# First half of the last head pair by way of DRAM, six taps on VectorE instead of TensorE, and a tile normalised and stored in two parts

## Chip, cores and metric

The kernel runs on one core of a Trainium2 chip. The metric is the device time of one execution in microseconds; the median of three runs is compared. All numbers are float32.

## What is computed

The input x is 16 images of 384 channels, 32 by 32 pixels. Two residual layers follow each other:

```
x = x + attention(gn(x))       # 8 heads of 48 channels over the 1024 pixels, softmax, projection, bias
x = x + depthwise_conv(gn(x))  # 7 x 7, padding 3, weights averaged over the four rotations
```

gn normalises groups of 12 channels over all pixels of an image. The convolution has one 7 x 7 filter for each channel: an output pixel is a sum of 49 products, and one of these 49 shifts (dy, dx) is called a tap.

## The kernel before

An image is three tiles of 128 channels by 1024 pixels. The work goes image by image; the convolution of an image runs beside the attention of the next one, on other engines.

Attention: the 8 heads are 4 pairs, so that there are 64 pairs in all (u = 0 to 63; pair 63 is the last of image 15). For each pair and each half of 512 query pixels, eight steps compute scores on TensorE (s_step, L493), ScalarE takes the exponential (L501), and eight steps multiply with v (av_step, L509). v has a column of ones, so that row 48 of each head's 64 rows of the result holds the softmax sum. ScalarE copies the result to the tile o (take, L520). Then o has to be divided by its sums. For the usual pair this goes by way of DRAM, in three steps that lie some microseconds apart: sums_out (L523) has SP write the two sum rows to DRAM and read them back spread over 128 partitions; invert (L532) takes the reciprocal of 16 columns on VectorE, and SP writes it to DRAM and reads it back, each head's row repeated over 64 partitions; divide (L543) multiplies on VectorE. For the last pair divide_at_once (L585) does it for a half in one go: a matmul with a matrix of ones copies the sums over the partitions (L588), VectorE takes the reciprocal of 512 columns (L590) and multiplies (L591). The first half is divided while TensorE projects the pairs 0 and 1 of the last image, the second half in fast_finish (L1274) between the projections of pair 2 and pair 3. After the projection come the residual (L608), the group statistics (groups_on_pe, L318: small matmuls with masks), and the convolution of the last image.

Convolution: a tap is one instruction on VectorE, x1 = x1 + w * shifted xn1 (conv_tap, L640; x1 is the accumulator, which begins as the layer's input, xn1 its normalised copy). Taps of different tiles take turns. Four helpers take work off VectorE. For the tiles in ROWS_ONLY some taps with dx = 0 are products on ScalarE (L621), which POOL adds in by an accumulating DMA (L945). Three tiles are convolved on TensorE, in PE_TILES: (14, 2), (15, 2) and (15, 1), written (image, tile). For these the normalised tile is stored to DRAM (conv_store, L714), read back four times shifted by a row (conv_load, L722), so that 32 channels by 4 rows lie on the 128 partitions, and multiplied with block matrices: one matmul step covers four values of dy for one dx (conv_on_pe, L756). PE_TAPS holds pairs (d0, dx) with d0 = 0 for dy from -3 to 0 and d0 = 1 for dy from 1 to 3. Each such pair is 4 matmuls for each half of 16 rows, and each matmul is two records in the profile. pe_taps leaves out (1, 0) for tile (14, 2), whose taps (1, 0), (2, 0) and (3, 0) are products on ScalarE. In the last image tile 0 has two accumulators (tap_of_two, L908), and sum3 collects its products.

Order: the schedule is manual. Two counters, clock for TensorE and vclock for VectorE, are advanced by written costs; catch_up (L967) fills VectorE with taps until vclock reaches clock, and runs what after(wait, cost, f) has put down once it is due. act_slot (L1078) does the same for what stands in applies on ScalarE. Each engine's queue, SP's and POOL's DMA starts among them, runs in the order in which the program issues it. SP carries sums, inverses and loads of shifted rows; POOL carries the accumulating DMAs and most stores of results; in the last image ScalarE starts half of the loads of shifted rows.

The turn to the last image's convolution is x1_chains (L1085). For image 15 VectorE normalises tile 2 (L360, conv_begin L632), SP stores it, ScalarE normalises tiles 1 and 0 (L364), and then products and taps of tile 0 begin. For image 14 the same function also queues the early products, each with its time. The tile pools hand out a fixed number of buffers in turn: six for x1, six for xn1, five for qk and the shifted rows, two for the inverses (tag "t"), three double banks and two single banks of PSUM.

Of the kernel before, what the change touches and what calls it, by code (L numbers as in the profile page):

```python
# [10 lines left out]
F32 = mybir.dt.float32  # L11
# [5 lines left out]
P = 128  # L17
# [27 lines left out]
def kernel(  # L45
# [64 lines left out]
    def run(general):  # L110
        tag = "g" if general else "f"
        with ExitStack() as stack:
# [33 lines left out]
            ROWS_ONLY[BESIDE] = range(-PAD, PAD + 1)  # L146

# [444 lines left out]

            def proj_part(b, o, ts):
                if o not in pps:
                    pps[o] = psum(f"ps_proj_{b}_{o}")
                for t in ts:
                    lhsT = wp[:, t, o * P : (o + 1) * P] if t < NK else late["w3"][:, o * P : (o + 1) * P]
                    for h in range(2):
                        nc.tensor.matmul(  # L599
                            pps[o][:, h, :],  # L600
                            lhsT=lhsT,
                            rhs=os_[NP * b + t][:, h * HALF : (h + 1) * HALF],
                            start=(t == 0),
                            stop=(t == NP - 1),
                        )
# [26 lines left out]
            def conv_begin(st, b, k, engine):  # L632
                xn1s[b, k] = spare.pop((b, k), None) or new_xn1(b, k)
                st.apply(xn1s[b, k], x1s[b, k], k, engine)
# [79 lines left out]
            def conv_store(b, k):  # L714
                nc.sync.dma_start(xds[b, k][:, PAD * W : (PAD + H) * W], xn1s[b, k])
# [20 lines left out]
            def pe_taps(b, k):  # L736
                return [t for t in PE_TAPS if t != (1, 0) or (b, k) not in ROWS_ONLY]
# [347 lines left out]
            def x1_chains(b, st):  # L1085
# [14 lines left out]
                if b == B - 2:  # L1100

                    vclock -= 5.0
# [3 lines left out]
                    early = [(beside, 0), (beside, -1), (beside, 1), (first, 1), (beside, -2)]  # L1106
# [46 lines left out]
            def finish(u):  # L1153
                sums_out(u)
                if u < U - 1:
                    waiting.add(u)
                    after(6.0 if u % NP == NP - 1 else 9.0, 0.3, lambda: finish2(u))
# [137 lines left out]
            def fast_end(b):  # L1295
                assert not applies
                for key in ("sum2", "sum3"):
# [13 lines left out]
            for b, n0, size in [  # L1311
# [15 lines left out]
                if ending:  # L1327
                    catch_up(clock)
                    divide_at_once(NP * b + NP - 1, 0)
                    vclock += 4.2  # L1330
# [13 lines left out]
                clock += (size * US_STEP + US_TURN) / 2  # L1344
                if n0 // (2 * NT) < (n0 + size) // (2 * NT):
                    finish((n0 + size) // (2 * NT) - 1)
                if ending:
                    catch_up(clock)
                    assert not invs and not waiting
# [94 lines left out]
```

## Time and profile before

| what | us |
|---|---|
| runs | 2911.31, 2907.84, 2912.79 |
| median | 2911.31 |
| profiled execution | 2906.68 |
| its span, first to last instruction | 2904.5 |

The busy time over the whole span, by engine (busy us, share, instructions):

```profile
PE 2894.4 (100%) x11446; PEld 1169.7 (40%) x11446; DVE 2565.6 (88%) x2559; ACT 1461.4 (50%) x1745; POOL 262.0 (9%) x411
```

PE is TensorE's matmuls, PEld its weight loads, DVE is VectorE, ACT is ScalarE, POOL is GpSimd. "DVE L640" is an instruction of line 640 on VectorE; SPq and ACTq are DMA starts in the queues of SP and ScalarE. The granted clock of TensorE was 1.0 of full speed. A few lines of the groups of instructions, with count, busy us and mean ns of one, then the idle time ahead and what ended most of it:

```profile
L640 DVE SCALAR_TENSOR_TENSOR x<-xn,wsym,x 128x930 f32<-128x930 f32 (+9 forms) x2170 | 2363.9, 1172 | 138.8 <-ACT xn L364 138.7
L756 PE MATMUL ps_conv<-sh,mat 128*32 128x480 f32 (+3 forms) x656 | 67.8, 569 | 0.0
L545 DVE TENSOR_TENSOR o<-o,inv 128x1024 f32<-128x1024 f32 x63 | 77.4, 1228 | 69.7 <-DMA inv<-inv 52.9
```

### The profile page before, as it was taken

To read this page: it belongs to the slowest core of one execution; us is meant where nothing else is said; L and a number is where in the kernel's file an instruction comes from. 1 tells how busy PE (TensorE), PEld (TensorE's weight loads), DVE (VectorE), ACT (ScalarE), POOL (GpSimd) and SP (SyncE) were. 2 spreads that over 40 slices of the span, in tenths; PEclk is the share of its full clock that TensorE was granted. 3 is DMA by queue.
4 is the path that set the end of the run, shared out by engine and by line. 5 is a ranking of instruction groups with operands and counts; after the bars stand their busy time and mean duration, and the time that the engine had idled before them with its cause. 6 is when DMAs were issued, how large, how long until landed. Compare 5 with 4: busy or idle time off the path is not lost.

```text
span 2904.5 us, 30161 instructions
## 1 busy us (share of the span) xinstructions
PE 2894.4 (100%) x11446; PEld 1169.7 (40%) x11446; DVE 2565.6 (88%) x2559; ACT 1461.4 (50%) x1745; POOL 262.0 (9%) x411
## 2 busy tenths in 40 slices
PE   9999999999999999999999999999999999999999
PEld 4343343433434343343433434343343433434333
DVE  5313999989899898998989899898998989899997
ACT  2546445464453645545465454645545455454641
POOL 3111004010100101000010100101001010100101
PEclk9999999999999999999999999999999999999999
DMA  7422022220312203012120212213022130212346
GB/s 287 131 26 63 16 36 77 38 67 23 65 33 43 70 21 84 16 35 70 35 71 16 65 41 43 67 24 84 16 36 70 28 77 16 55 50 43 83 125 174
DMA packets 74284, 175.80 MB, mean 61 GB/s; under 512 B 30528, under 2 KB 32464, under 8 KB 72592
## 3 DMA queue, kind: packets, MB, share of 16 engines
q0 software_dynamic: 34336, 114.90, 15.9%
q1 hardware_dynamic: 38080, 55.20, 7.6%
q10 hardware_dynamic: 1712, 3.67, 0.4%
q8 instruction: 92, 1.51, 0.2%
q14 instruction: 64, 0.52, 0.1%
HBM read 118.61 MB, written 28.72 MB: 51 GB/s over the span
## 4 chain that ended last, share of the span: by engine, by line
PE 100%; DVE 0%; ACT 0%; POOL 0%; issue 0%; POOLq 0%
PE ps_s L493 31%; PE acc L509 31%; PE ps_qk L442 17%; PE ps_v L468 9%; PE ps_proj L562 8%; PE ps_conv L756 2%; PE ps_proj L599 1%; PE warm L1182 0%; PE ps_st_x L332 0%; PE ps_sum L588 0%; ACT qk L449 0%; POOL sc_x L353 0%; DVE x L360 0%; DVE x L777 0%; DVE ones_warm L1176 0%
## 5 line engine op out<-in xcount | busy, mean ns | idle before, releaser
L640 DVE SCALAR_TENSOR_TENSOR x<-xn,wsym,x 128x930 f32<-128x930 f32 (+9 forms) x2170 | 2363.9, 1172 | 138.8 <-ACT xn L364 138.7
L501 ACT ACTIVATE e<-ps_s 128x1024 f32<-128x1024 f32 x1024 | 952.5, 1051 | 54.5 <-PE ps_s L493 51.6
L493 PE MATMUL ps_s<-qk 48*128 48x512 f32 x4096 | 914.2, 596 | 1.1 <-ACT qk L449 1.1
L509 PE MATMUL acc<-e,v 128*64 128x512 f32 x4096 | 907.2, 595 | 0.0
L493 PEld LDWEIGHTS ps_s<-qk 48*128 48x128 f32 x4096 | 376.5, 185 | 535.0 <-ACT e L501 257.2
L509 PEld LDWEIGHTS acc<-e,v 128*64 128x64 f32 x4096 | 283.0, 137 | 608.2 <-issue 599.7
L442 PE MATMUL ps_qk<-x,wqk 128*128 128x512 f32 x1152 | 505.7, 595 | 1.0 <-DVE x L360 1.0
L520 ACT COPY o<-acc 128x512 f32<-128x512 f32 x128 | 75.2, 587 | 602.5 <-PE acc L509 602.3
L442 PEld LDWEIGHTS ps_qk<-x,wqk 128*128 128x128 f32 x1152 | 216.1, 190 | 287.1 <-issue 285.7
L468 PE MATMUL ps_v<-wv,x 128*128 128x384 f32 x768 | 252.0, 488 | 0.0
L562 PE MATMUL ps_proj<-o,wp 128*128 128x512 f32 x540 | 234.2, 592 | 0.0
L449 ACT COPY qk<-ps_qk 128x1024 f32<-128x1024 f32 x96 | 96.8, 1009 | 254.1 <-PE ps_qk L442 254.1
L577 POOL DMA_DIRECT2D x<-in_x x45 | 39.3, 872 | 1796.7 <-ACT x L570 1423.1
L468 PEld LDWEIGHTS ps_v<-wv,x 128*128 128x128 f32 x768 | 144.6, 190 | 109.7 <-ACT e L501 12.1
L562 PEld LDWEIGHTS ps_proj<-o,wp 128*128 128x128 f32 x540 | 102.6, 190 | 126.0 <-issue 120.3
L477 ACT COPY v<-ps_v 128x384 f32<-128x384 f32 x128 | 55.1, 483 | 185.6 <-PE ps_v L468 185.6
L570 ACT ACTIVATE x<-ps_proj,bp 128x1024 f32<-128x1024 f32 x45 | 50.2, 1115 | 182.7 <-PE ps_proj L562 182.7
L545 DVE TENSOR_TENSOR o<-o,inv 128x1024 f32<-128x1024 f32 x63 | 77.4, 1228 | 69.7 <-DMA inv<-inv 52.9
L364 ACT ACTIVATE xn<-x,sc_x 128x1024 f32<-128x1024 f32 x47 | 54.9, 1231 | 71.6 <-DMA sc_x<-gr_x 62.4
L756 PE MATMUL ps_conv<-sh,mat 128*32 128x480 f32 (+3 forms) x656 | 67.8, 569 | 0.0
L387 DVE BATCH_NORM_STATS2 bs_all<-xs 128x6 f32<-128x512 f32 x84 | 52.1, 682 | 17.3 <-DMA xs<-in_x 17.1
L458 POOL DMA_DIRECT2D qk<-qk x96 | 47.3, 526 | 116.4 <-ACT qk L449 115.4
(143 smaller groups left out, 565.4 us busy)
## 6 DMA issues: line engine op xcount, KB each, us to landing
x<-in_x POOLq DMA_DIRECT2D x90, 512.0 KB, 5.6
inv<-inv SPq DMA_DIRECT2D x126, 256.0 KB
out<-x POOLq DMA_DIRECT2D x45, 512.0 KB, 3.8
xs<-in_x POOLq DMA_DIRECT2D x42, 512.0 KB, 6.1
qk<-qk POOLq DMA_DIRECT2D x96, 128.0 KB, 5.9
o<-o SPq DMA_DIRECT2D x90, 64.0 KB
sh<-xd SPq DMA_DIRECT2D x32, 160.0 KB
x<-in_x SPq DMA_DIRECT2D x6, 512.0 KB
```

The source lines that it names most:

```text
L442: nc.tensor.matmul(ps[:, h, :], lhsT=wqk[:, k, s, t, :], rhs=xns[b][:, k, h * HALF : (h + 1) * HALF], start=(k == 0), stop=(k == NK - 1),)
L449: nc.scalar.copy(halves(qks[u][:, s, :]), ps)
L468: nc.tensor.matmul(ps[:, j, 0:C], lhsT=xns[b][:, k, t * P : (t + 1) * P], rhs=wv[:, k, :], start=(k == 0), stop=(k == NK - 1),)
L477: nc.scalar.copy(dst.rearrange("p (h d) -> p h d", d=D + 1)[:, :, 0:D], ps[:, j, 0:C].rearrange("p (h d) -> p h d", d=D),)
L493: nc.tensor.matmul(ps[:, j, :], lhsT=qks[u][r, 1, i * P : (i + 1) * P], rhs=qks[u][r, 0, h * HALF : (h + 1) * HALF], start=True, stop=True,)
L501: nc.scalar.activation(es[n], ps, AF.Exp, scale=SCALE)
L509: nc.tensor.matmul(accs[u, h][64 * j : 64 * j + 64, :], lhsT=v_of(u, i, j), rhs=e[:, j, :], start=(i == 0), stop=(i == NT - 1),)
L520: nc.scalar.copy(os_[u][:, h * HALF : (h + 1) * HALF], accs.pop((u, h)))
L545: nc.vector.tensor_tensor(os_[u], os_[u], invs.pop(u), ALU.mult)
L562: nc.tensor.matmul(ps[:, h, :], lhsT=wp[:, t, o * P : (o + 1) * P], rhs=os_[NP * b + t][:, h * HALF : (h + 1) * HALF], start=(t == 0), sto ...
L640: nc.vector.scalar_tensor_tensor(acc, xn1s[b, k].rearrange("p (h w) -> p h w", w=W)[:, iy, ix], wsym[:, k, dy + PAD, dx + PAD : dx + PAD + 1],
L756: nc.tensor.matmul(dst[CH * i : CH * (i + 1), :].rearrange("p (y x) -> p y x", x=W)[:, :, ox], lhsT=mats[k][:, i, d0 * KS + dx + PAD, :], ...
```

## The change

Four things are changed.

- half_sums, half_invert and half_divide are new and do for the first half of pair 63 what the other pairs do by way of DRAM; they begin one group of steps before the end of the pair. divide_at_once is called for the second half alone, and vclock is not advanced by 4.2 for it. sums_out of the last pair moves from finish to fast_end.
- pe_taps leaves out (1, -1) and (1, 1) too for tile (14, 2). The six taps, dy from 1 to 3 with dx -1 and 1, are done by VectorE in aside, ahead of the tile's products.
- Tile (15, 2) is normalised in two instructions, the first 20 rows and the last 12, and stored by two DMAs: SP starts the first, ScalarE the second.
- vclock is set back by 3 instead of 5 at the turn of image 14, and in the list of early products (14, 0) with dy = -2 and (14, 2) with dy = 1 change places.

```diff
--- before.py
+++ after.py
@@ -144,6 +144,8 @@
 
             BESIDE = None if general else (B - 2, 0)
             ROWS_ONLY[BESIDE] = range(-PAD, PAD + 1)
+
+            ASIDE = (1, -1)
 
             def taps_of(b, k):
                 return [t for t in TAPS if t[1] or t[0] not in ROWS_ONLY.get((b, k), ())]
@@ -590,6 +592,32 @@
                 nc.vector.reciprocal(inv, ps)
                 nc.vector.tensor_tensor(half, half, inv, ALU.mult)
 
+
+            def half_sums(u):
+                sum_d = ddram.tile([2, HALF], F32, tag="sumh", name=f"sumh_{u}")
+                for j in range(2):
+                    r = 64 * j + D
+                    nc.sync.dma_start(sum_d[j : j + 1, :], os_[u][r : r + 1, 0:HALF])
+                late["sumh"] = small.tile([P, SC // 2], F32, tag="sumh", name=f"sumh_{u}")
+                nc.sync.dma_start(late["sumh"], sum_d.rearrange("j (p c) -> (j p) c", c=SC // 2))
+                after(4.0, 0.3, lambda: half_invert(u))
+
+            def half_invert(u):
+                nc.vector.reciprocal(late["sumh"], late["sumh"])
+                inv_d = ddram.tile([2, HALF], F32, tag="invh", name=f"invh_{u}")
+                nc.sync.dma_start(inv_d.rearrange("j (p c) -> (j p) c", c=SC // 2), late["sumh"])
+                inv = tpool.tile([P, N], F32, tag="t", name=f"invh_{u}")[:, 0:HALF]
+                for j in range(2):
+                    nc.sync.dma_start(
+                        inv[64 * j : 64 * j + 64, :], inv_d[j : j + 1, :].to_broadcast([64, HALF])
+                    )
+                after(7.5, 0.7, lambda: half_divide(u, inv))
+
+            def half_divide(u, inv):
+                half = os_[u][:, 0:HALF]
+                nc.vector.tensor_tensor(half, half, inv, ALU.mult)
+                late["half"] = True
+
             def proj_part(b, o, ts):
                 if o not in pps:
                     pps[o] = psum(f"ps_proj_{b}_{o}")
@@ -631,7 +659,12 @@
 
             def conv_begin(st, b, k, engine):
                 xn1s[b, k] = spare.pop((b, k), None) or new_xn1(b, k)
-                st.apply(xn1s[b, k], x1s[b, k], k, engine)
+                if (b, k) == PE_TILES[1] and not general:
+                    n = (ROWS - PAD + SH - 1) * W
+                    st.apply(xn1s[b, k][:, 0:n], x1s[b, k][:, 0:n], k, engine)
+                    st.apply(xn1s[b, k][:, n:], x1s[b, k][:, n:], k, engine)
+                else:
+                    st.apply(xn1s[b, k], x1s[b, k], k, engine)
 
             def conv_tap(b, k, dy, dx, dst=None):
                 (oy, iy), (ox, ix) = region(dy, dx)
@@ -712,7 +745,13 @@
                 vclock += 2.2
 
             def conv_store(b, k):
-                nc.sync.dma_start(xds[b, k][:, PAD * W : (PAD + H) * W], xn1s[b, k])
+
+                cuts = (0, ROWS - PAD + SH - 1, H) if (b, k) == PE_TILES[1] else (0, H)
+                for y0, y1 in zip(cuts, cuts[1:]):
+                    queue = nc.scalar if y0 else nc.sync
+                    queue.dma_start(
+                        xds[b, k][:, (PAD + y0) * W : (PAD + y1) * W], xn1s[b, k][:, y0 * W : y1 * W]
+                    )
 
             def conv_load(b, k, h, a):
 
@@ -734,7 +773,7 @@
             PE_TAPS.sort(key=lambda t: t[1] != 0)
 
             def pe_taps(b, k):
-                return [t for t in PE_TAPS if t != (1, 0) or (b, k) not in ROWS_ONLY]
+                return [t for t in PE_TAPS if (b, k) not in ROWS_ONLY or not t[0] or t[1] not in (0, *ASIDE)]
 
             def conv_on_pe(b, k, h, first, last):
                 if (b, k) == PE_TILES[-1]:
@@ -1099,11 +1138,18 @@
                     after(2.5, 0.0, lambda: lone_rows(*LONE))
                 if b == B - 2:
 
-                    vclock -= 5.0
+                    vclock -= 3.0
                     for k in range(NK):
                         spare[B - 1, k] = new_xn1(B - 1, k)
                     beside, first = BESIDE, PE_TILES[0]
-                    early = [(beside, 0), (beside, -1), (beside, 1), (first, 1), (beside, -2)]
+
+                    def aside():
+                        for dy in range(1, PAD + 1):
+                            for dx in ASIDE:
+                                conv_tap(*first, dy, dx)
+
+                    after(1.0, 7.0, aside)
+                    early = [(beside, 0), (beside, -1), (beside, 1), (beside, -2), (first, 1)]
                     early += [(first, 2), (beside, 2), (first, 3), (beside, -3), (beside, 3)]
                     for n, (bk, dy) in enumerate(early):
                         applies.append(
@@ -1151,8 +1197,8 @@
             waiting = set()
 
             def finish(u):
-                sums_out(u)
                 if u < U - 1:
+                    sums_out(u)
                     waiting.add(u)
                     after(6.0 if u % NP == NP - 1 else 9.0, 0.3, lambda: finish2(u))
 
@@ -1294,6 +1340,7 @@
 
             def fast_end(b):
                 assert not applies
+                sums_out(U - 1)
                 for key in ("sum2", "sum3"):
                     late[key] = opool.tile([P, N], F32, tag="o", name=key)
                 nc.gpsimd.memset(late["sum3"][:, N - W :], 0.0)
@@ -1326,8 +1373,6 @@
                 ending = b == B - 1 and r + size == PER_B
                 if ending:
                     catch_up(clock)
-                    divide_at_once(NP * b + NP - 1, 0)
-                    vclock += 4.2
                     for o in range(NK):
                         proj_part(b, o, (0, 1))
                     loads(1)
@@ -1342,11 +1387,13 @@
                     if i == NT - 1:
                         take(u, h)
                 clock += (size * US_STEP + US_TURN) / 2
+                if b == B - 1 and r + 2 * size == PER_B:
+                    half_sums(n0 // (2 * NT))
                 if n0 // (2 * NT) < (n0 + size) // (2 * NT):
                     finish((n0 + size) // (2 * NT) - 1)
                 if ending:
                     catch_up(clock)
-                    assert not invs and not waiting
+                    assert not invs and not waiting and late["half"]
                     fast_finish(b)
                 else:
                     other(n0 + size, True)
```

## Prediction

> **What bounds the kernel now.** I read the chain that ended last first, then busy time by stage over the last 200 us, then the timeline of VectorE and of the queues there, and last the order of both programs' instructions. That order is the same on every engine up to VectorE's taps of image 13, at 2706 us; nothing before can change.
>
> The chain of waits, last part (start us, length us, what):
>
> ```profile
> 2789.98 7.07 PE ps_s L493 x32
> 2797.05 1.05 PE ps_sum L588 x2
> 2798.10 10.30 PE ps_proj L599 x24
> ...
> 2836.36 61.64 PE ps_conv L756 x596
> 2898.00 0.03 issue
> 2898.03 0.69 DVE x L777
> ```
>
> TensorE works without a gap until 2898.00; one add of half a tile and its store end the kernel. By stage (busy us of PE, PEld, DVE, ACT, POOL):
>
> ```profile
> 2705.00:2797.00 92.00, 92.00 (x397) 34.35 (x393) 89.09 (x90) 61.96 (x68) 14.02 (x21) 1.00 0.61 151
> 2797.00:2827.00 30.00, 30.00 (x90) 11.90 (x92) 29.57 (x25) 3.37 (x6) 0.70 (x2) 1.00 0.14 41
> 2827.00:2852.00 25.00, 24.97 (x242) 9.80 (x246) 20.78 (x36) 11.04 (x13) 2.36 (x3) 1.00 0.49 137
> 2852.00:2898.00 46.00, 45.98 (x448) 18.09 (x440) 39.76 (x40) 2.03 (x2) 5.76 (x7) 1.00 0.79 192
> ```
>
> VectorE is nearly as full. Its timeline shows how little is left, and where it stood:
>
> ```profile
> 2771.41 1.23 DVE L545 TENSOR_TENSOR o<-o,inv 128x1024 f32<-128x1024 f32 x1 [2.30 <-ACT xn L621]
> 2800.08 3.35 DVE L590 RECIPROCAL inv<-ps_sum 128x512 f32<-128x512 f32 x1
> 2818.23 3.36 DVE L590 RECIPROCAL inv<-ps_sum 128x512 f32<-128x512 f32 x1 [0.16 <-PE ps_sum L588]
> 2822.29 2.25 DVE L640 SCALAR_TENSOR_TENSOR x<-xn,wsym,x 128x841 f32<-128x841 f32 x2
> 2840.18 2.13 DVE L640 SCALAR_TENSOR_TENSOR x<-xn,wsym,x 128x841 f32<-128x841 f32 x2 [0.53 <-ACT xn L364]
> 2890.82 1.22 DVE L918 TENSOR_TENSOR sum<-sum,sum 128x1024 f32<-128x1024 f32 x1 [2.06 <-DMA sum<-tap_-3_13772]
> 2898.03 0.69 DVE L777 TENSOR_TENSOR x<-ps_conv,x 128x512 f32<-128x512 f32 x1 [4.18 <-PE ps_conv L756]
> ```
>
> In brackets is the idle time ahead. So VectorE has 4.18 us to TensorE's end and 2.06 us more for a transfer: 6.2 us of slack. ScalarE and SP in the last turn:
>
> ```profile
> 2837.78 2.37 ACT L364 ACTIVATE xn<-x,sc_x 128x1024 f32<-128x1024 f32 x2 [9.25 <-DVE sc_x L354]
> 2838.62 0.81 SPq L715 DMA_DIRECT2D xd<-xn  x2
> 2841.71 3.03 ACTq L722 DMA_DIRECT2D sh<-xd  x4
> ```
>
> [...] one conv record lasts 569 ns, but 596 take 61.64 us, 103 ns each; I price by 103. [...] Here sum<-o at 2816.08 lets its dependent start at 2817.64 (1.6 us), at a loaded moment 4.4. [...] Pair 61's broadcast, issued at 2760.61 beside POOL's accumulating transfers, was read at 2771.41; pair 60's second part, issued at 2727.03, at 2731.58. [...] the trace has 3.35 us against 0.69 for a multiply of the same 512 columns.
>
> **Part 1, two taps off TensorE.** (1,-1) and (1,1) of tile (14,2) go: 2 taps x 4 matmuls x 2 halves, two records each, 32 records x 103 ns = 3.3 us. Six taps of 961, 930 and 899 elements, twice each, come on VectorE, 1.13, 1.10 and 1.06 us from start to start (from neighbours in the timeline): 6.6. They all write one tile; the two such taps at 2822.29 took 2.17 to the next start instead of 1.01 + 1.03, so 0.12 for each of five pairs: 7.2 us. They stand at 2706.7, ahead of image 13's last four taps. ScalarE's first product, at 2709.59, waits for one of these and so for about 2715.5. Behind it stands the qk copy that TensorE made ready at 2714.4; it comes at 2716.6. The next scores take another pair's qk and the third PSUM buffer; TensorE does not stand. Image 13's three stores on POOL slide 6 us, next to qk's copies; that delays pair 60's broadcast.
>
> **Part 2, half of pair 63 by way of DRAM.** Removed: ps_sum, 1.05 us of TensorE, and a reciprocal, 3.45 us from start to start (2800.08 to 2803.53). Added: on VectorE a reciprocal of 8 columns, 0.17 (as of 16, 2721.38 to 2721.55); the multiply stays. On SP six transfers. The sums leave at 2790.6 (ScalarE's copy ends), are back at about 2794, and stand ahead of pair 62's two steps, which come 3 us later than now but are wanted only at 2797 or later. The inverse goes out behind four sh loads, about 2797, and is broadcast at 2798.5 to 2799.7, to land near 2802.5. The multiply comes up at 2802.5 to 2805, TensorE wants it at 2820. I take no wait; bounds 0 and 2 us. The sh load behind waits 3 us more and is read at 2838.
>
> **Part 3, the two parts of (15,2).** VectorE: 0.73 becomes about 0.9. SP's store of 20 rows starts 0.3 earlier and is smaller; before, the sh loads began 3.0 us after it. But the second store is issued by ScalarE, ahead of both normalisations: it waits for VectorE's second part (0.95 instead of 0 after sc_x) and takes about 0.4 to issue. So xn of (15,0) comes 1.35 us later (bounds 0.9 and 1.6). Queued behind: both products, ScalarE's four sh loads, and VectorE's first tap of (15,0), with only one tap as filler.
>
> **Part 4, vclock and the order of products.** The order lists show six taps of image 14 moved behind each of the multiplies of pairs 60 and 61, two behind the last reciprocal, L901 behind the statistics, and three more taps left after sc_x. Removing L777's first half from the end costs nothing.
>
> **The sum.** D is the lateness of the last reciprocal against 2818.23. To the multiply of pair 61: 7.2 - 6 taps x 1.05 = +0.9, less the 0.6 idle at pair 60. If the broadcast of pair 61 lands as before, VectorE leaves there at 2771.41 as now. Behind it: six taps 6.3, -3.45 + 0.17, two taps -2.04, L901 -1.14 = -0.2, where 0.16 was idle: D = 0. Pair 60's broadcast behind the moved stores may bring 0.5 to 3; the wait at pair 61 absorbs part. I take D = 0.7 (bounds -1.05, where TensorE's ps_sum comes first, and 3). TensorE wants the second half's inverse right after its third projection, so its 1.05 us is lost there for every D above -1.05.
>
> VectorE then: first tap of (15,0) at 2840.18 + 1.4 + D; from there to the last tap's end 48.6 us now (2888.8), and three taps more, 3.2; then L777 0.6, L918 1.14 (the transfers it waits for move forward with TensorE's conv), L924 1.2. L777's last half starts at 2896.3 + D = 2897.0. TensorE: 2898.0 - 3.3 + D + 0.4 for sh loads = 2895.8. VectorE is last. 2897.0 against 2898.03 is -1.0 us; the three last stores now stand within 2 us, at most +0.6, which I leave in the range. The profiled execution took 2906.68 us (span 2904.5, 2.2 around it), the median of three runs is 2911.31; the difference carries over: 2911.31 - 1.0 = 2910.3.
>
> **Rivals.**
> - TensorE's savings arrive whole: -3.3 - 1.05 = -4.4 us, 2906.9. For it: the chain is TensorE at all points. Against: 6.2 us of slack, of which the six taps less the reciprocal take 3.9 and the late xn 1.4, and the last reciprocal was not waiting for more than 0.16. Chance 0.12.
> - The split does not start the loads sooner. SP's half does begin early, ScalarE's half 1.3 us late; TensorE reaches tile (15,2) 3.3 us earlier than 2851.7, with some 3 us of margin now. If it stands 3 us there, TensorE ends at 2898.4: +0.4 us, 2911.7. Chance 0.13.
> - Slower: VectorE, in order, stands at four multiplies in a row (pairs 60, 61, 62, half 63), each behind a broadcast that shares the DMA engines with POOL's transfers. If each costs the 2.3 us of pair 61, D rises by 7 to 9 and everything behind slides: -1.7 + 8 = +6.3 us, 2917.6. It is slower than now from D = 1.7. Against: DMA is busy only 0.14 of the time from 2797 on. Chance 0.13, most of it at small D.
> - The forecast, VectorE last by a little: 0.62.
>
> **How the numbers follow.** A change of 0.2% (5.8 us) is what a measurement of this kernel can tell from none. More gain than 4.4 us is not in the change, so faster by that much is left to scatter (the three runs span 5 us): 0.05. Slower needs D over 7.5: 0.08. Within: 0.87. The forecast's own range is -3.2 (D = -1.05 and the lower bound of part 3) to +1.9 (D = 3, stores 0.6); with scatter of the median, and the first rival, 2906.2; upwards, with part of the slow case, 2915.0.
>
> **What would show it.** 624 conv records instead of 656; no idle of VectorE ahead of the last L777, with TensorE's end 1 us or more before it; the reciprocal of the second half within 2 us of 2818; ScalarE's normalisation about 1.3 us after sc_x; idle before the first tap of (15,0) of 1.5 to 2 us instead of 0.53. I am wrong if TensorE still ends the chain, if idle of over 2 us stands ahead of the multiplies of pairs 60 to 63, or if TensorE shows idle at 2847.

## The result, and the profile after

The changed kernel takes 2914.03 us (median of 22 runs, 2912.26 to 2917.79), the kernel before 2908.98 us in runs on the same chip (median of 22, 2906.23 to 2912.79). The ratio is 1.0018, 95% interval 1.0012 to 1.0024: some 5 us slower, where the forecast had said 1.0 us faster.

The profiled execution of the changed kernel has a span of 2912.8 us (2904.5 before). Some of that is older than the change: its first 100 us ran at a granted clock of 0.98 instead of 1.00, and SP issues the sums of pair 60 (before, then changed kernel) 2.0 us later:

```profile
2709.72 0.54 SPq L527 DMA_DIRECT2D sum<-o  x2
2711.74 0.53 SPq L529 DMA_DIRECT2D sum<-o  x2
```

So what follows is counted, where it matters, from that issue, which I call A in each execution. Both profiles are of one execution each; that of the kernel before took 2906.68 us, 2.3 less than the median of that kernel.

First the chain of waits of the changed kernel, the whole of it (start, us, what):

```profile
2902.92 0.09 issue
2903.01 1.23 DVE sum L957
2904.24 0.02 issue
2904.26 0.70 DVE x L963
2904.97 0.06 DVEq L1445
2905.02 0.15 DVE x L963
2905.17 0.30 issue
2905.48 0.68 DVE x L816
```

Before, TensorE's conv stood at the end of it. Now VectorE does, and the chain can't be followed further back than its last adds, so it doesn't tell where the time went. The stretches do (us from start to end; then busy us of PE, PEld, DVE, ACT, POOL; granted clock; DMA share; GB/s):

```profile
2705.00:2797.00 92.00, 92.00 (x398) 34.25 (x395) 84.51 (x85) 60.42 (x67) 14.60 (x23) 1.00 0.56 138
2797.00:2827.00 30.00, 26.65 (x82) 10.35 (x80) 30.00 (x29) 4.20 (x5) 0.00 (x0) 1.00 0.27 71
2827.00:2852.00 25.00, 22.97 (x165) 9.85 (x169) 17.18 (x27) 6.56 (x10) 1.46 (x2) 0.87 0.18 68
2852.00:2898.00 46.00, 45.67 (x450) 19.65 (x446) 45.97 (x52) 7.66 (x8) 7.24 (x9) 1.00 0.89 207
```

Three things differ from the same stretches before. VectorE stands 7.5 us in the first (2.9 before). TensorE, which had no gap, lacks 3.4 us in the second and 2.0 in the third. And in the third its clock was 0.87. The timelines of VectorE (three lines) and TensorE (two) give the places; idle time ahead stands in brackets:

```profile
2739.23 1.23 DVE L547 TENSOR_TENSOR o<-o,inv 128x1024 f32<-128x1024 f32 x1 [5.54 <-ACT e L503]
2778.13 1.23 DVE L547 TENSOR_TENSOR o<-o,inv 128x1024 f32<-128x1024 f32 x1 [1.71 <-issue]
2824.82 3.36 DVE L592 RECIPROCAL inv<-ps_sum 128x512 f32<-128x512 f32 x1
...
2829.03 6.87 PE L627 MATMUL ps_proj<-o,mat 128*128 128x512 f32 x10 [5.38 <-DVE o L593]
2858.56 45.88 PE L795 MATMUL ps_conv<-sh,mat 128*32 128x512 f32 x444 [0.33 <-DMA sh<-xd]
```

The same multiply in the kernel before:

```profile
2731.58 1.23 DVE L545 TENSOR_TENSOR o<-o,inv 128x1024 f32<-128x1024 f32 x1 [0.61 <-issue]
```

VectorE stands 5.54 us ahead of pair 60's multiply (0.61 before). The releaser named there, an exponential of ScalarE, is only the last semaphore that the profile saw; what the multiply lacks is the inverse: the last packet of its broadcast ends 26.5 us after A, and the multiply starts at 27.5. The last reciprocal starts 113.1 us after A instead of 108.5: D, the lateness on which the forecast hung, is 4.6 us. TensorE stands 5.38 us for what that reciprocal makes, and then its ten projection records take 6.87 us instead of 4.56 at full clock.

Why the inverse is late is seen on ScalarE, POOL and SP, all in the changed kernel:

```profile
2717.98 1.15 ACT L649 ACTIVATE xn<-xn,wsym 128x1024 f32<-128x1024 f32 x1 [6.26 <-DVE x L673]
2719.03 1.00 ACT L451 COPY qk<-ps_qk 128x1024 f32<-128x1024 f32 x1
2719.92 1.12 ACT L649 ACTIVATE xn<-xn,wsym 128x992 f32<-128x992 f32 x1
...
2720.19 0.53 POOL L684 DMA_DIRECT2D out<-x  x1 [0.45 <-DVE x L673]
2721.35 0.87 POOL L984 DMA_DIRECT2D xn<-xn  x1 [0.63 <-ACT xn L649]
2721.91 3.21 POOL L460 DMA_DIRECT2D qk<-qk  x6
...
2724.33 0.34 SPq L538 DMA_DIRECT2D inv<-rec  x1
2731.44 1.13 SPq L541 DMA_DIRECT2D inv<-inv  x2
```

And in the kernel before:

```profile
2709.59 1.15 ACT L621 ACTIVATE xn<-xn,wsym 128x1024 f32<-128x1024 f32 x1
2715.35 1.13 ACT L621 ACTIVATE xn<-xn,wsym 128x992 f32<-128x992 f32 x1
...
2716.78 0.87 POOL L945 DMA_DIRECT2D xn<-xn  x1 [5.10 <-ACT xn L621]
...
2721.64 0.34 SPq L536 DMA_DIRECT2D inv<-rec  x1
2726.49 1.12 SPq L539 DMA_DIRECT2D inv<-inv  x2
```

ScalarE's first product waits 6.26 us for a tap of VectorE; a qk copy, which starts 7.3 us after A without a wait of its own (4.7 before), and the second product are behind it; POOL's accumulating add needs the second product, and qk's copies stand behind that add on POOL. SP sends pair 60's reciprocals to DRAM at 2724.33, and only 7.1 us later (4.9 before) can it issue their broadcast, that is, the read that repeats each head's row over 64 partitions. The packets of the DMA queues in the two traces, in us after A:

```
                                   before     changed kernel
POOL's add, 3968-byte packets      8 to 11    11 to 15
qk's copies, 8192-byte packets     11 to 16   14 to 19
pair 60's inverse, 64-byte         14 to 16   16 to 19
its broadcast, 4096-byte           18 to 21   21 to 27
POOL's next add, 3968-byte         21 on      22 to 26
```

The 64-byte packets move when the copies are nearly through. They are 3 us late, and so the broadcast, which before ended just as the next add began, now runs into it and takes 5.0 us instead of 3.1: 3 us of slip become 5.6 at the multiply.

### The profile page after: what moved, and what is told of

It reads as the page before. It is cut to its first block, busy times and chain, and to the rows that moved or that the text cites. A ratio compares the mean times of both kernels' runs of the same rounds, so it can differ in the third digit from the quotient of the medians.

```text
span 2912.8 us, 30111 instructions
## 1 busy us (share of the span) xinstructions
PE 2896.1 (99%) x11412; PEld 1172.9 (40%) x11412; DVE 2570.0 (88%) x2566; ACT 1461.6 (50%) x1745; POOL 262.1 (9%) x411
## 5 line engine op out<-in xcount | busy, mean ns | idle before, releaser
L673 DVE SCALAR_TENSOR_TENSOR x<-xn,wsym,x 128x899 f32<-128x899 f32 (+9 forms) x2176 | 2369.9, 1164 | 141.0 <-ACT xn L366 140.8
L795 PE MATMUL ps_conv<-sh,mat 128*32 128x464 f32 (+3 forms) x624 | 65.1, 569 | 0.3 <-DMA sh<-xd 0.3
L366 ACT ACTIVATE x<-x,x_sc 128x1024 f32<-128x1024 f32 x42 | 51.1, 1270 | 19.2 <-DMA x<-in_x 19.2
```

Of the source, the lines that this page charges most:

```text
L366: nc.scalar.activation(dst, src, AF.Identity, bias=self.sc[:, k, 1:2], scale=self.sc[:, k, 0:1],)
L673: nc.vector.scalar_tensor_tensor(acc, xn1s[b, k].rearrange("p (h w) -> p h w", w=W)[:, iy, ix], wsym[:, k, dy + PAD, dx + PAD : dx + PAD + 1],
L795: nc.tensor.matmul(dst[CH * i : CH * (i + 1), :].rearrange("p (y x) -> p y x", x=W)[:, :, ox], lhsT=mats[k][:, i, d0 * KS + dx + PAD, :], ...
```

## The experiments

Each kernel ran in turns with the kernel before on the same chip. The table sums up the profiles, one execution of each kernel (waits of VectorE ahead of the multiplies of pairs 60, 61 and 62; TensorE's stand ahead of pair 63's second half; start of that half's multiply after A) and the times (ratio to the kernel before, 95% interval; it differs by up to 0.0004 from the quotient of the medians that the text gives). Waits under 0.35 us are shown as a dash.

| kernel | 60 | 61 | 62 | TensorE stands | multiply after A | ratio |
|---|---|---|---|---|---|---|
| before | 0.61 | 2.30 | - | - | 112.0 | 1 |
| changed | 5.54 | 1.71 | - | 5.38 | 116.5 | 1.0018 (1.0012 to 1.0024) |
| e1 taps late | 1.17 | 3.68 | - | 3.21 | 114.4 | 1.0004 (0.9995 to 1.0012) |
| e2 stores by ScalarE | 4.75 | 1.05 | - | 4.35 | 115.5 | 1.0014 (1.0008 to 1.0021) |
| e3 stand filled | 4.83 | 1.12 | - | 0.35 | 115.7 | 1.0009 (1.0001 to 1.0018) |
| e4 no part 1 | 0.68 | 4.19 | - | 2.80 | 114.0 | 1.0000 (0.9992 to 1.0008) |
| e5 stores late | 5.14 | 1.52 | - | 4.72 | 115.9 | 1.0017 (1.0010 to 1.0024) |
| e6 multiplies late | - | - | 2.48 | 1.34 | 112.5 | 0.9996 (0.9988 to 1.0005) |
| e7 e1 and e6 | - | - | 2.12 | 1.36 | 112.5 | 0.9994 (0.9985 to 1.0002) |
| e8 e7, store by POOL | - | - | 3.07 | 1.28 | 112.4 | 0.9991 (0.9982 to 0.9999) |
| e9 products late | - | 1.09 | 1.34 | 1.30 | 112.9 | 1.0000 (0.9991 to 1.0008) |
| e10 e8, sums aside | - | - | - | 0.74 | 112.3 | 0.9992 (0.9985 to 0.9999) |
| e11 part 1 alone | 2.92 | 2.87 | - | 5.31 | 117.3 | 1.0019 (1.0012 to 1.0027) |
| e12 e10, half later | - | - | - | - | 111.6 | 0.9987 (0.9980 to 0.9993) |

### Whose place, and whose load: e1, e2, e3, e4

The theory after reading the traces: the six taps stand at the wrong place and hold back what image 13's last tap releases. The rivals: 7.2 us more are too much for VectorE wherever they stand; or the DRAM half and the store that ScalarE issues cost the time.

**e1** moves the six taps behind image 13's last four:

```diff
-                    after(1.0, 7.0, aside)
+                    after(6.0, 7.0, aside)
```

> The six taps of tile (14,2) stand behind image 13's last four taps instead of ahead of them; the same instructions otherwise. Order theory (the taps hold back image 13's stores, whose traffic on POOL's queue holds back pair 60's inverse): ScalarE's first product back within 1 us of the kernel before's place (0.2 to 0.6 idle instead of 6.3), the wait ahead of pair 60's multiply falls from 5.5 us to under 1.5, TensorE's stand ahead of the last projections from 5.4 us to under 2, its granted clock stays at 1.00 behind it; 5 to 7 us less than the changed kernel, 0 to 2 us less than the kernel before (ratio 0.9992 to 1.0002). Load theory (7.2 us more on VectorE, wherever they stand): TensorE still stands 4 to 6 us, ratio as the changed kernel's 1.0018. Theory of the DRAM half and the ScalarE store: also 1.0018.

2910.85 us against 2908.62. By the medians 2.8 of the 5 us are gone, by the ratios 4, with no instruction fewer, so the load alone isn't the loss. ScalarE's first product is back, and pair 60's multiply waits 1.17 us (ScalarE, then VectorE, in the profile of e1):

```profile
2710.88 1.15 ACT L649 ACTIVATE xn<-xn,wsym 128x1024 f32<-128x1024 f32 x1
...
2733.33 1.23 DVE L547 TENSOR_TENSOR o<-o,inv 128x1024 f32<-128x1024 f32 x1 [1.17 <-DMA inv<-inv]
2775.23 1.23 DVE L547 TENSOR_TENSOR o<-o,inv 128x1024 f32<-128x1024 f32 x1 [3.68 <-issue]
```

The gain over the kernel before did not come: TensorE stands 3.21 us, more than the 2 expected, because pair 61's multiply waits 3.68 us in this execution (more on that wait under e4).

**e2** lets ScalarE issue image 13's three stores, at the same moment:

```diff
-                (nc.scalar if b == B - 1 and not general else nc.gpsimd).dma_start(
+                (nc.scalar if b in (B - 3, B - 1) and not general else nc.gpsimd).dma_start(
```

> The six taps stay where the change put them; image 13's three stores are issued by ScalarE instead of POOL, at the same moment. If POOL's queue is what holds the small packets of pair 60's inverse [...], the wait ahead of pair 60's multiply falls from 5.5 to 1 to 3 us and the time by 3 to 6 us (ratio 0.9997 to 1.0008). If it is the bytes themselves on the DMA engines, whatever the queue, the wait stays at 4 to 6 us and the ratio at 1.0015 to 1.002.

The wait is 4.75 us, as in the second branch, and the ratio 1.0014, a little under it. The 64-byte packets of pair 60's inverse move 16 to 19 us after A, as in the changed kernel. So it isn't the length of POOL's queue that the stores add to. Whether it is the stores at all, e5 asks.

**e3** puts five matmuls into TensorE's stand, behind the first of pair 63's projections:

```diff
                             stop=(t == NP - 1),
                         )
+                        if (o, t, h) == (0, NP - 1, 0):
+                            ps = ps_o.tile([P, HALF], F32, tag="acc", name="ps_fill")
+                            for _ in range(5):
+                                nc.tensor.matmul(
+                                    ps,
+                                    lhsT=late["masks"][:, 7, :],
+                                    rhs=os_[NP * b][:, 0:HALF],
+                                    start=True,
+                                    stop=True,
+                                )
```

> Five matmuls whose result is read by nothing are put into TensorE's stand ahead of pair 63's second half (4.4 of its 5.4 us); nothing else differs. If TensorE's clock fell because it stood, the granted clock stays at 1.00 through the last projections, the wait of the residual behind them (1.8 us) goes, and the kernel gains 2 to 2.5 us against the changed kernel (ratio 1.0009 to 1.0012). If the clock falls for another reason, or is off the path, the ratio stays at 1.0018 (or rises by up to 0.5 us).

2911.35 us, ratio 1.0009: useless work made the kernel faster, by half of its loss. TensorE's timeline in e3, and then the stretch behind the stand (columns as for the stretches above):

```profile
2823.16 4.45 PE L637 MATMUL ps_fill<-o,masks 128*128 128x512 f32 x10
2827.97 4.56 PE L627 MATMUL ps_proj<-o,mat 128*128 128x512 f32 x10 [0.35 <-DVE o L593]
```

```profile
2827.00:2852.00 25.00, 24.65 (x200) 10.05 (x202) 19.29 (x36) 9.87 (x13) 2.36 (x3) 1.00 0.32 102
```

The ten records take 4.56 us again instead of 6.87, the clock is 1.00 instead of 0.87. The second half's multiply is as late as in the changed kernel, within 0.8 us. So some 2.3 us of the loss by the medians, 2.6 by the ratios, are the clock that fell at the stand. The intervals of the two ratios overlap a little; the trace says the same, though: from the last reciprocal to the two-part normalisation the changed kernel takes 2.2 us more than the kernel before, e3 0.1 us less.

**e4** undoes part 1 and its order:

```diff
-                return [t for t in PE_TAPS if (b, k) not in ROWS_ONLY or not t[0] or t[1] not in (0, *ASIDE)]
+                return [t for t in PE_TAPS if t != (1, 0) or (b, k) not in ROWS_ONLY]
...
-                    vclock -= 3.0
+                    vclock -= 5.0
...
-                    def aside():
-                        for dy in range(1, PAD + 1):
-                            for dx in ASIDE:
-                                conv_tap(*first, dy, dx)
-
-                    after(1.0, 7.0, aside)
-                    early = [(beside, 0), (beside, -1), (beside, 1), (beside, -2), (first, 1)]
+                    early = [(beside, 0), (beside, -1), (beside, 1), (first, 1), (beside, -2)]
```

> Part 1 and its order undone (TensorE has its 32 records again, VectorE no six taps, products and budget as before); the DRAM half and the two-part store stay. Order and load theories: pair 60's wait under 1.5 us, TensorE does not stand, last reciprocal 2 to 4 us earlier than the changed kernel's; 0.5 to 3 us less than the kernel before (ratio 0.999 to 0.9998). Theory of the DRAM half or the ScalarE store: 3 to 6 us over the kernel before stay (1.001 to 1.002).

2909.46 us, ratio 1.0000, and in the profiled execution TensorE stands:

```profile
2825.76 6.26 PE L627 MATMUL ps_proj<-o,mat 128*128 128x512 f32 x10 [2.80 <-DVE o L593]
```

The DRAM half and the two-part store together neither cost nor gain, as far as an interval of 2.3 us to either side tells. Pair 61's multiply waits 4.19 us here where the kernel before shows 2.30, although up to there both programs issue the same instructions in the same order on VectorE, ScalarE, POOL and SP. So this wait can differ by 2 us between executions of the same instructions. The traces show with what it goes together: SP sends pair 61's reciprocals to DRAM at about the time at which POOL issues two accumulating adds and other transfers (us from the first of these adds to SP's issue, and from that to SP's broadcast of the inverse):

```
                         SP after POOL    until the broadcast
e6, e9, e10, e12         -0.4 to -0.1     1.5
e7, e8                   0.1              1.5
before                   0.3              1.5
e4                       0.65             4.1
e1                       1.4              6.7
changed, e2, e3, e5, e11 5.0 to 6.5       5.5 to 6.8
```

A few tenths of a microsecond seem to decide, though no run shifts this issue alone. The kernel before was profiled on the short side; e4, whose order is the same, on the long one. And VectorE's stand at pair 60 makes pair 61's reciprocals late too, which puts them behind the add.

### Stores, or products: e5 and e9

**e5** leaves the taps ahead and sends image 13's stores two adds later:

```diff
             def conv_end(b, k):
-
+                if b == B - 3 and not general:
+                    after(26.0, 0.0, lambda: store_late(b, k))
+                    return
+                store_late(b, k)
+
+            def store_late(b, k):
```

> The six taps stay ahead of image 13's last four, but image 13's three stores go out two accumulating adds later, behind qk's copies; nothing else moves. Order theory as the packets of the first four runs tell it (the stores push the product's add and qk's copies 3 us back, the 64-byte packets of pair 60's inverse move only when those are through, and then meet the next add): the wait ahead of pair 60's multiply falls from 5.5 to 0.5 to 2 us, TensorE's stand from 5.4 to under 3 us; ratio 1.0000 to 1.0008. If the cause is ScalarE's late product and qk copy themselves, not the stores: the wait stays at 4 to 6 us, ratio 1.0014 to 1.002.

The theory as the expectation puts it is wrong: 2914.07 us, ratio 1.0017, and the wait stays. POOL's timeline in e5 shows why:

```profile
2720.32 0.95 POOL L989 DMA_DIRECT2D xn<-xn  x1 [16.11 <-ACT xn L649]
2720.89 3.29 POOL L460 DMA_DIRECT2D qk<-qk  x6
```

Nothing is ahead of the add on POOL any more, and it is still issued 9.6 us after A, as in the changed kernel (7.1 in the kernel before), because it waits for ScalarE's second product. The stores are not what holds pair 60's inverse.

**e9** tests what is left: ScalarE's first two products, and so POOL's first add, go behind both qk copies:

```diff
-                                clock + 2.0 + 7.0 * n,
+                                clock + max(2.0 + 7.0 * n, 18.0),
```

> The changed kernel (six taps ahead, stores where they were, multiplies where they were), but ScalarE's first two products stand behind the two qk copies and eight exponentials, and so POOL's first add behind qk's copies. If the chain is: six taps, then ScalarE's first product (it waits for image 13's last tap), then the second product, POOL's add, qk's copies behind it on POOL, and behind their packets the inverse, then the copies go out before the inverse is ready: its 64-byte packets leave within 2 us of their issue, the wait ahead of pair 60's multiply is under 1 us; TensorE's stand under 3 us; ratio 1.0000 to 1.0010. If the DMA engines are simply full at that time: wait 3 to 6 us, ratio 1.0012 to 1.002.

2908.43 us against 2908.76, ratio 1.0000, with the six taps and the stores where the change put them. POOL, SP and VectorE in e9:

```profile
2720.20 2.96 POOL L460 DMA_DIRECT2D qk<-qk  x6
2731.79 0.92 POOL L984 DMA_DIRECT2D xn<-xn  x1 [8.63 <-ACT xn L649]
...
2723.80 0.34 SPq L538 DMA_DIRECT2D inv<-rec  x1
2727.95 1.13 SPq L541 DMA_DIRECT2D inv<-inv  x2
...
2733.07 1.22 DVE L547 TENSOR_TENSOR o<-o,inv 128x1024 f32<-128x1024 f32 x1
```

The copies go out ahead of the add, the inverse needs 4.15 us on its way (its 64-byte packets leave 2.0 to 3.4 us after their issue, not within 2: the copies' packets run until 16 us after A), its broadcast ends before the next add, and the multiply does not wait. That is the chain: six taps, first product, second product, add, qk's copies, inverse.

### Waiting, or the lateness itself: e6, e7, e8

**e6** leaves the inverse late and lets the multiplies of pairs 60 and 61 come five taps later:

```diff
-                after(5.5 if u % NP == NP - 1 else 9.5, 1.3, lambda: finish3(u))
+                after(5.5 if u % NP == NP - 1 else 15.0 if u in (U - 4, U - 3) else 9.5, 1.3, lambda: finish3(u))
```

> The changed kernel with the multiplies of pairs 60 and 61 five taps (some 5.5 us) later in VectorE's order; the inverses arrive as late as in the changed kernel. If standing at these two multiplies is the whole loss: both waits together under 1.5 us instead of 7.2, last reciprocal 4 to 6 us earlier, TensorE stands under 1 us and keeps its clock, and what the forecast had promised comes out: 1 to 3.5 us less than the kernel before (ratio 0.9988 to 0.9997). Load theory (7.2 us of taps are too much for VectorE): no idle anywhere and still 1.0010 to 1.0018.

2907.35 us against 2909.28, ratio 0.9996: by the ratios some 6.4 us less than the changed kernel, with all its instructions and with the inverse as late as there. Both waits are gone, TensorE stands 1.34 us (under 1 was expected), and its clock stays at 1.00. So VectorE can carry the six taps; what it can't afford is to stand. Pair 61's inverse, with no stand at pair 60 ahead of it, also leaves ahead of POOL's add again. A new wait shows behind (VectorE, then TensorE, in e6):

```profile
2798.83 1.23 DVE L547 TENSOR_TENSOR o<-o,inv 128x1024 f32<-128x1024 f32 x1 [2.48 <-DMA inv<-inv]
2822.99 4.56 PE L627 MATMUL ps_proj<-o,mat 128*128 128x512 f32 x10 [1.34 <-DVE o L593]
```

It is pair 62's multiply, and it comes from part 2: SP takes that pair's reciprocals only 6 us after they are made, since the half's sums stand ahead of them on SP.

**e7** joins the edits of e1 and e6:

> Both remedies: the six taps behind image 13's last four, and the two multiplies five taps later. Neither wait over 0.5 us, last reciprocal where TensorE's sum allows it, ratio 0.9986 to 0.9996. If it is no better than the later multiplies alone, TensorE's sum for the second half or VectorE's own load is what bounds then.

2907.72 us, ratio 0.9994: no better than e6, as far as intervals of 2.5 us to either side tell. With nobody standing at pair 60, the place of the taps no longer counts. Pair 62 waits as in e6, which the expectation had not seen.

**e8** adds to e7 that POOL issues the second part of the two-part store:

```diff
-                    queue = nc.scalar if y0 else nc.sync
+                    queue = nc.gpsimd if y0 else nc.sync
```

> As the last, and the second part of the two-part store issued by POOL instead of ScalarE. ScalarE's normalisation of (15,0) then starts 0.1 to 0.3 us after sc_x instead of 1.5. If VectorE's last stretch is the end of the kernel, another 1.0 to 1.4 us less than the run before it (0.9982 to 0.9992); if TensorE is, less than 0.5; if POOL's store lands too late for the loads behind it, TensorE stands 1 to 3 us at tile (15,2) and the run is slower than the one before it.

2906.47 us, ratio 0.9991, 1.25 us under e7, which is less than the intervals can tell apart. The mechanism is plain, though (ScalarE's normalisation and VectorE's first tap of (15,0) in e8; sc_x starts at 2840.20):

```profile
2840.40 2.37 ACT L366 ACTIVATE xn<-x,sc_x 128x1024 f32<-128x1024 f32 x2 [9.28 <-DVE sc_x L356]
...
2842.80 2.16 DVE L673 SCALAR_TENSOR_TENSOR x<-xn,wsym,x 128x841 f32<-128x841 f32 x2 [0.37 <-ACT xn L366]
```

In e7 the normalisation starts 1.7 us after sc_x and the tap has 1.88 us of idle ahead.

### Towards a better kernel: e10, e12; and part 1 alone: e11

**e10** is e8 with the half's sums sent by ScalarE and fetched by POOL:

```diff
                     r = 64 * j + D
-                    nc.sync.dma_start(sum_d[j : j + 1, :], os_[u][r : r + 1, 0:HALF])
+                    nc.scalar.dma_start(sum_d[j : j + 1, :], os_[u][r : r + 1, 0:HALF])
...
-                nc.sync.dma_start(late["sumh"], sum_d.rearrange("j (p c) -> (j p) c", c=SC // 2))
+                nc.gpsimd.dma_start(late["sumh"], sum_d.rearrange("j (p c) -> (j p) c", c=SC // 2))
```

> The best kernel so far (taps later, multiplies later, second store on POOL) with the half's sums sent out by ScalarE and fetched by POOL instead of SP, so that pair 62's inverse no longer stands behind them on SP (6.1 to 6.9 us from reciprocal to issue in the last three runs). Pair 62's inverse is issued within 1 us of its reciprocal, the wait of 2 to 3 us ahead of its multiply goes, TensorE stands under 0.4 instead of 1.3 us; 0.8 to 1.8 us less than the run before it (ratio 0.9982 to 0.9990). If SP's order costs nothing because TensorE is the bound: the same as that run.

2906.65 us, ratio 0.9992: the wait at pair 62 went, as expected, and nothing was gained, since another took its place (VectorE in e10):

```profile
2800.44 0.20 DVE L606 RECIPROCAL sumh<-sumh 128x8 f32<-128x8 f32 x1 [3.42 <-DMA sumh<-sumh]
```

The half's own reciprocal now waits for POOL's fetch, in front of work that could go on. **e12** moves it four taps down, which TensorE, that wants the half some 20 us later, doesn't notice:

```diff
-                after(4.0, 0.3, lambda: half_invert(u))
+                after(8.5, 0.3, lambda: half_invert(u))
```

> As the last but one kernel (taps and multiplies later, second store on POOL, the half's sums by ScalarE and POOL), with the half's own reciprocal four taps later in VectorE's order, so that it no longer stands 3.4 us for POOL's fetch. No wait over 0.5 us on VectorE between 2710 and the last reciprocal; TensorE's stand at the second half under 0.3 us instead of 0.7; TensorE is then the bound, so only 0.3 to 1.0 us less than that kernel: ratio 0.9984 to 0.9993. If the four sh loads that now stand ahead of the half's inverse on SP hold it up, its multiply waits 1 to 3 us and nothing is gained.

2905.62 us against 2908.69, ratio 0.9987, interval 0.9980 to 0.9993: faster than the kernel before and the changed kernel. (From e10 to e12 it is 1.0 to 1.5 us, which the intervals can't tell apart.) The last reciprocal now waits for TensorE, no longer TensorE for it (VectorE in e12), and TensorE's conv ends the kernel again:

```profile
2820.90 3.36 DVE L592 RECIPROCAL inv<-ps_sum 128x512 f32<-128x512 f32 x1 [2.43 <-PE ps_sum L590]
...
2898.59 0.69 DVE L816 TENSOR_TENSOR x<-ps_conv,x 128x512 f32<-128x512 f32 x1 [0.76 <-PE ps_conv L795]
```

**e11** is the kernel before with part 1 alone. Its edit is e4's turned round, but the planner's budget stays at 5.0:

```diff
+            ASIDE = (1, -1)
...
-                return [t for t in PE_TAPS if t != (1, 0) or (b, k) not in ROWS_ONLY]
+                return [t for t in PE_TAPS if (b, k) not in ROWS_ONLY or not t[0] or t[1] not in (0, *ASIDE)]
...
-                    early = [(beside, 0), (beside, -1), (beside, 1), (first, 1), (beside, -2)]
+                    def aside():
...
+                    after(1.0, 7.0, aside)
+                    early = [(beside, 0), (beside, -1), (beside, 1), (beside, -2), (first, 1)]
```

> The kernel before with part 1 alone (two taps of TensorE's first tile on VectorE, products in the new order, the planner's budget left at the old 5.0); no DRAM half, no two-part store. Order theory: a wait of 4 to 6 us ahead of pair 60's multiply here too, last reciprocal 4 to 7 us later than before, ratio 1.0010 to 1.0025. If the loss needs the DRAM half or the two-part store: no wait over 2 us, ratio 0.9990 to 1.0005.

2913.97 us against 2908.76, ratio 1.0019: part 1 alone costs as much as the whole change. Its waits at pairs 60 and 61 are 2.92 and 2.87 us, not 4 to 6 at the first: with the other budget the six taps stand ahead of image 13's last two taps instead of four, so ScalarE's first product isn't held, and its second only by 1.40 us. The chain runs here all the same: image 13's last two stores and then the add go out on POOL, the add 8.9 us after A and pair 60's broadcast 19.4 us (7.1 and 16.8 before, 9.6 and 19.7 in the changed kernel). The second half's multiply is 5.3 us late all the same, of which the two waits are 2.9 (5.79 together, 2.91 before) and the rest, by subtraction, tap time that no shorter reciprocal pays for here. So part 1 is enough for the loss, but how it splits into waits and tap time is another matter in each kernel.

## Why the prediction was wrong

The measured 2914.03 us lies near the slow end of the stated range; the point, 2910.3, and the direction were wrong.

**The step that failed** is the size of D: "Pair 60's broadcast behind the moved stores may bring 0.5 to 3; the wait at pair 61 absorbs part. I take D = 0.7". The wait at pair 60 grew by 4.9 us (5.54 against 0.61), pair 61 gave back 0.6, and D was 4.6. The upper bound of 3 was too low because it counted one slip. It had the forecast's own facts at hand: ScalarE's first product at 2715.5 (measured 2717.98, or 2716.0 without the 2.0 us by which A is later), the qk copy behind it at 2716.6 (2717.0 counted so). What it did not follow was the second product behind that copy, to the add and qk's copies on POOL, and from the end of those to the next add. The "loaded moment 4.4" that it quotes is SP's wait for pair 60's own reciprocals in the kernel before: the transfer that it then left out of the sum.

**Its cause was misnamed.** It was to be image 13's stores, "next to qk's copies". Moving the stores to another queue (e2) or out of the way (e5) left the wait; moving the products (e9) or the taps (e1) removed it.

**A term was missing.** TensorE's stand was not only lost time: its clock fell to half at it, for 6.8 us by the record. The prediction had shown TensorE waiting for the last half for every D above -1.05 and took the wait alone, which put the clock at nothing without a reason. e3 prices the clock at 2.3 to 2.6 us; in the trace, the two-part normalisation comes another 2.2 us later against A than D explains.

**The sum with the measured terms** nearly holds: -1.7 + D for the start of VectorE's last add, that is -1.7 + 4.6 = 2.9, and 2.2 for the clock: 5.1 us. In the two profiles that add starts 5.4 us later against A, and the program ends 6.3 later: behind it the stores and the end took 0.8 us more, where the range had 0.6. That 5.1 is so near to the 5.05 between the medians is in part luck, since the profiled executions are not the median ones.

**What held.** 624 conv records, as counted. The six taps took 7.2 us in a row. Without the waits VectorE's way to the last reciprocal grew by 0.4 us, where the sum had 0.7. VectorE is last: no idle ahead of the last L816, and TensorE's conv, 2858.56 + 45.88, ends 1.0 us before it starts. ScalarE's normalisation is late by the store that it issues: 1.7 us after sc_x, where 1.3 had been named, and the first tap of (15,0) with 1.88 us of idle (0.53 before), where it was 1.5 to 2; e8 removes it. Part 2 saved its reciprocal (0.21 us for the small one) with no wait in the changed kernel. That pair 62's steps, behind the half's transfers on SP, were wanted late enough was right only because everything was late: in e6 to e8 they cost 2 to 3 us.

**The rivals.** The slower one had the right mechanism, VectorE in order behind a late broadcast, and the right point, slower from D = 1.7. It expected 2.3 us at each of four multiplies; it was 4.9 at one. It got 0.13, because DMA's low share from 2797 on spoke against it; but the place was some 60 us earlier, in a stretch where that share was 0.61 before and is 0.56 now. That TensorE's savings arrive whole, or that it stands for loads at tile (15,2) (0.33 us), didn't happen.

## What to carry to other kernels

7.2 us of taps, put on VectorE ahead of the last use of a tile, delayed here everything that waits for the tile: ScalarE's first product stood for 6.26 us, and the last reciprocal came 4.6 us later. Follow such a release through every engine and queue to the end, not to the first neighbour, and ask at the end what the late transfer runs into. Where the data are wanted much later, put the consumer further down in the waiting engine's order before trying to speed up the transfer: e6 gained 6.4 us by that, and no rerouting tried here (e2, e8, e10) gained more than some 1.3 us. TensorE stands of 2.80 to 5.38 us cost 1.7 to 2.8 us on top of the stand here, by the ten records behind them.

## What the runs showed of the hardware

- **The clock was lower behind some of the stands.** Stands of 2.80 us (e4) and 3.21 us (e1) are followed by 3.4 us at granted clock 0.5, by the traces' clock records. At stands of 4.35 to 5.38 us (e2, e5, e11, changed kernel) the record has 6.8 us at 0.5; in the changed kernel the first 2.1 of them still lie in the stand. After stands of 1.28 to 1.36 us (e6 to e9) and after 4.45 us filled with useless matmuls (e3) it stays at 1.00. The ten records behind the stand take 6.26 us (e4), 6.25 (e1), 6.95 (e2), 7.32 (e5), 7.29 (e11) and 6.87 (changed kernel) against 4.56. The difference is half of the 3.4 us in e4 and e1, and half of 6.8 - 2.1 in the changed kernel. Ahead of pair 63's second half no stand between 1.36 and 2.80 us was seen, so from what length on the clock falls was not shown.
- **Small packets went late beside large ones.** From SP's start of one pair's reciprocals (128 packets of 64 bytes) to its start of the broadcast that waits for them it took 1.5 us in e7 for pair 62, and 7.1 us beside qk's copies and the add (changed kernel, pair 60). For pair 61 it took 1.5 us where the issue came at most 0.3 us after that of POOL's add (before, e6 to e10, e12), and 4.1 to 6.8 us where it came 0.65 us or more after it. Pair 60's 64-byte packets moved only when most of the 8192-byte packets were through (changed kernel: half of the small ones start later than 18.1 us after A, nine in ten of the large ones earlier), and with another queue for the stores (e2) they moved no earlier, 16 to 19 us after A. What decides this order inside the DMA engines was not shown.
